# Graph attention in column tiles of 32: four narrow matmuls in place of one wide one, in a two-layer graph kernel

## The chip, the cores and the metric

The kernel runs on one core of a Trainium2 chip. The metric is the device time of one execution in microseconds, the median over a few runs. One execution is also taken with the hardware profiler; it gives the profile and the trace that this document reads.

## The reference

Two layers follow each other on a graph of N = 2708 nodes with 512 features. Only the first is touched here. It normalises x, takes the positive part h, and applies graph attention with 8 heads of 64 features over a dense adjacency matrix of zeros and ones. Cut to what matters:

```python
feats = jnp.einsum('nf,hfd->hnd', X, W)
e_self = jnp.einsum('hnd,hd->hn', feats, a_self)
e_neigh = jnp.einsum('hnd,hd->hn', feats, a_neigh)
dense = e_self[:, :, None] + e_neigh[:, None, :]
dense = jnp.where(dense >= 0, dense, LEAKY_ALPHA * dense)
dense = dense + (NEG_INF * (1.0 - A))[None, :, :]
attn = jax.nn.softmax(dense, axis=-1)
out = jnp.einsum('hnm,hmd->hnd', attn, feats) + b[:, None, :]
out = jnp.transpose(out, (1, 0, 2)).reshape(N, H * D)
return jax.nn.relu(out)
```

The layer's result is added to x. The second layer (graph diffusion in two steps, with a nucleus mask found by a search for thresholds) takes the larger part of the time and stays as it is.

## The kernel before

The nodes are cut into NT = 22 row tiles of 128 (the last has 20 rows). Everything that is multiplied here is f32.

**First stage.** Per row tile, x is normalised and projected. The tile `fw[:, t, head, :]` gets 65 columns for each head (DV = DH + 1): the 64 features times exp(e_neigh), and in the last column exp(e_neigh) itself, so that one matmul gives a head's weighted sum of features and the sum of its weights. `kk` holds exp(-0.8 e_neigh), and the tensor `en_d` in memory exp(0.8 e_self). A weight of the attention is then max(en, kk) times the adjacency, up to a factor that cancels.

**Attention.** The destination nodes are cut into chunks of whole row tiles, at most four (`tchunks`): six chunks, four of 512 columns, one of 384, one of 276. A chunk loads the share `r_b` of four heads at a time (line 345), broadcast to all partitions, and all 22 tiles of the transposed adjacency for its columns into `a_c` (line 434, f32, NT + 2 buffers). ScalarE copies each of them to `s_c` (line 439), which adds its row sums on the way and is stored to `s_d` for the second layer. For the nodes of the chunk, whole rows of the adjacency are loaded into `arow` and summed on ScalarE (`row_sums`, lines 338 and 339).

Then, for each of the two groups of four heads, for each row tile t, for each head of the group: VectorE writes the weights `e`, which are the larger of r_b and kk, times a_c (line 455, 10 buffers), and TensorE multiplies them into that head's bank of PSUM (line 457), accumulating over t:

```python
po = [ps_o.tile([P, 512], F32, name="po")[:DV] for _ in grp]
...
nc.tensor.matmul(po[i][:, :cw], lhsT=fw[:pr, t, hd, :], rhs=e[:pr, :cw],
                 start=(t == 0), stop=(t == NT - 1))
```

Six banks serve `po` and two the transposes. After the 22 tiles ScalarE copies the four banks to `o_t` (line 462), 65 partitions for each head.

**Finishing.** Each finished row tile of a chunk passes five stages (`finished`): `turned` transposes o_t per head (line 366), `shared` divides by the sums of weights, `normed` adds x and normalises, `cleared` takes the positive part, `asked` projects for the second layer (transposes on line 412, matmuls on line 175). These stages are put behind row tiles of the next chunk (`later`), one at a time, so that they run between its matmuls. The last chunk has no next one: its stages follow at the end (`final`), and the last of them is left to the beginning of the second layer.

**Order.** In this part the framework lays out each engine's order in advance; loads and stores are issued by SyncE in one queue, and each engine carries out its instructions in that order. Waits come from the tiles: an instruction that writes a buffer waits for the last reader of what stood there.

Of the kernel before, what the change touches and what calls it, by code (L numbers as in the profile page):

```python
# [9 lines left out]
F32 = mybir.dt.float32  # L10
BF16 = mybir.dt.bfloat16
# [13 lines left out]
P = 128  # L25
# [28 lines left out]
def kernel(  # L54
# [157 lines left out]
    NB = -(-NT // TG)  # L212
    tchunks = []
    for c in range(NB):
        t0 = tchunks[-1][-1] + 1 if c else 0
        tchunks.append(list(range(t0, t0 + NT // NB + (c < NT % NB))))
    with ExitStack() as l0:
# [110 lines left out]
        tp = l0.enter_context(tc.tile_pool(name="l0t", bufs=10))  # L328
# [14 lines left out]
        def shares(grp, n0, cw):  # L343
            r_b = rbp.tile([P, HG, 512], F32, name="r_b")
# [6 lines left out]
        def finished(t, o_t, c0, bank, final):  # L351
# [3 lines left out]
            f3 = fsum.rearrange("p (h d) -> p h d", h=H)  # L355
# [12 lines left out]
            def shared():  # L368
# [5 lines left out]
                for pn, grp in zip(pns, hgroups):  # L374
                    nc.vector.tensor_scalar(den[:pr, grp[0]:grp[-1] + 1], pn[:pr, :, DH],
                                            lone_n[:pr, t:t + 1], None, op0=OP.add)
                nc.vector.reciprocal(rden[:pr], den[:pr])
                for pn, grp in zip(pns, hgroups):
                    s = slice(grp[0], grp[-1] + 1)
                    nc.vector.scalar_tensor_tensor(o3[:pr, s, :], f3[:pr, s, :], lone[:pr, t:t + 1],  # L380
                                                   pn[:pr, :, :DH], op0=OP.mult, op1=OP.add)
# [44 lines left out]
        for ci, tiles in enumerate(tchunks):  # L426
# [1027 lines left out]
```

## Time and profile before

| what | us |
|---|---|
| median of 3 runs (lowest to highest) | 3573.36 (3570.47 to 3583.9) |
| the profiled execution | 3562.47 |
| its span in the trace | 3560.7 |
| TensorE busy, matmuls (10797 records) | 3332.0 (94%) |
| TensorE weight loads busy | 1729.1 (49%) |
| VectorE busy | 2650.8 (74%) |
| ScalarE busy | 1508.6 (42%) |
| GpSimd busy | 890.4 (25%) |
| transfers | 579.99 MB, mean 163 GB/s |

A line of the page's fifth part reads: source line, engine, operation, tile written, tiles read, shape, number; then busy us and mean ns of one; then the idle time of the engine just before such instructions, and what ended most of it. PE stands for matmuls, PEld for weight loads, DVE for VectorE, ACT for ScalarE, POOL for GpSimd, SP for SyncE. `128*65 128x512` at a matmul means 128 rows by 65 columns of weights, and 512 moving columns from 128 partitions. In the second part the span is cut into 40 slices of 89 us, and each digit is a busy share in tenths. Matmul records contain the time in which the array empties, so the records of successive matmuls overlap.

### The profile page before, as it was taken

The numbers are of one execution on the slowest core, as the hardware profiler recorded it, in microseconds if no ns is written. First come the engines' busy times: TensorE is split into PE (matmuls) and PEld (weight loads), VectorE is DVE, ScalarE is ACT, GpSimd is POOL, SyncE is SP. The second block draws the span as 40 slices with busy tenths as digits, with TensorE's granted clock in tenths as the row PEclk, the third lists the DMA queues.
The fourth block names the chain that finished last, engine by engine and source line by source line (L and its number), as shares of the span: only waits on it lengthen the run. The fifth ranks groups of instructions, "written<-read, shape, count | busy, mean of one in ns | idle before, by whom it ended". The sixth has DMA issues, their size and how long they took to land. (4 is left out here: it accounts for less than half of the span.)

```text
span 3560.7 us, 34129 instructions
## 1 busy us (share of the span) xinstructions
PE 3332.0 (94%) x10797; PEld 1729.1 (49%) x10797; DVE 2650.8 (74%) x4828; ACT 1508.6 (42%) x2269; POOL 890.4 (25%) x1074
## 2 busy tenths in 40 slices
PE   8999999998988999999999999899998999988998
PEld 4433333333455544646555554465555555555554
DVE  4587888889985756545464734598899998888883
ACT  2344211111103676566565642353655554545610
POOL 4114241415321121211222221311312332212211
PEclk9999999999999999999999999999999999999999
DMA  4476424242327624525344453695545535556453
GB/s 116 155 244 243 154 95 139 76 125 84 103 98 269 238 83 153 196 90 208 108 157 170 136 175 101 226 307 169 175 163 189 199 130 183 174 183 210 163 202 124
DMA packets 251348, 579.99 MB, mean 163 GB/s; under 512 B 33945, under 2 KB 76553, under 8 KB 248291
## 3 DMA queue, kind: packets, MB, share of 16 engines
q1 hardware_dynamic: 229063, 503.39, 42.7%
q0 software_dynamic: 22064, 74.09, 5.4%
q8 instruction: 86, 1.41, 0.2%
q14 instruction: 135, 1.11, 0.1%
HBM read 471.68 MB, written 105.68 MB: 162 GB/s over the span
## 5 line engine op out<-in xcount | busy, mean ns | idle before, releaser
L1140 PE MATMUL a<-va,at 128*128 128x512 f32 (+2 forms) x1936 | 887.1, 598 | 5.0 <-ACT at L1122 4.7
L457 PE MATMUL po<-e,fw 128*65 128x512 f32 (+4 forms) x2112 | 841.9, 554 | 28.8 <-DVE e L455 20.4
L455 DVE SCALAR_TENSOR_TENSOR e<-r_b,kk,a_c 128x512 f32<-128x512 f32 (+4 forms) x1056 | 750.4, 739 | 70.0 <-PE po L457 19.0
L576 ACT ACTIVATE junk_a<-p,nth 128x2708 uint8<-128x2708 f32 (+1 forms) x240 | 612.8, 2553 | 32.1 <-POOL nth L591 27.6
L1014 PE MATMUL q<-hl,s_r 128*128 128x512 f32 x1936 | 537.9, 424 | 63.3 <-DMA s_r<-s_d 45.3
L457 PEld LDWEIGHTS po<-e,fw 128*65 128x65 f32 (+1 forms) x2112 | 287.3, 140 | 543.5 <-issue 275.1
L1140 PEld LDWEIGHTS a<-va,at 128*128 128x128 f32 (+2 forms) x1936 | 338.3, 186 | 374.5 <-issue 341.9
L1014 PEld LDWEIGHTS q<-hl,s_r 128*128 128x128 f32 x1936 | 363.5, 192 | 225.9 <-issue 64.8
L1122 ACT COPY at<-t 128x512 f32<-128x512 f32 (+3 forms) x308 | 140.6, 478 | 655.8 <-PE t L1118 652.4
L655 DVE SCALAR_TENSOR_TENSOR junk<-p,th 128x2708 bf16<-128x2708 f32 (+1 forms) x132 | 407.2, 3085 | 3.0
L1034 PE MATMUL q<-u_k,v 128*128 128x512 f32 x704 | 316.9, 592 | 0.8 <-ACT v L1024 0.8
L1017 PE MATMUL q<-s_r,hl 128*128 128x512 f32 (+1 forms) x1056 | 282.3, 413 | 15.2 <-DMA s_r<-s_d 11.1
L1017 PEld LDWEIGHTS q<-s_r,hl 128*128 128x128 f32 x1056 | 196.0, 192 | 94.9 <-issue 51.6
L1034 PEld LDWEIGHTS q<-u_k,v 128*128 128x128 f32 x704 | 133.3, 190 | 158.6 <-issue 154.4
L544 ACT COPY p<-t 128x452 f32<-128x452 f32 (+2 forms) x264 | 131.3, 536 | 162.0 <-PE t L542 115.6
L542 PE MATMUL t<-keys,q_t 128*128 128x452 f32 x528 | 160.9, 432 | 41.2 <-ACT p L544 38.1
L851 DVE MAX8 vn<-keep 128x8 f32<-128x2708 f32 (+1 forms) x66 | 196.8, 2981 | 2.3
L569 DVE TENSOR_REDUCE nmx<-p 128x1 f32<-128x2708 f32 (+1 forms) x44 | 130.5, 2967 | 88.1 <-ACT p L544 88.1
L439 ACT ACTIVATE s_c<-a_c 128x512 fp32r<-128x512 f32 (+3 forms) x132 | 76.2, 577 | 249.0 <-DMA a_c<-in_adj_t_dram 122.3
L1187 PE MATMUL a<-u_k,v_t 128*128 128x512 f32 (+1 forms) x352 | 168.6, 619 | 5.2 <-ACT yo L1194 3.0
L1118 PEld LDWEIGHTS t<-ident,keep 128*128 128x128 f32 (+1 forms) x968 | 114.7, 139 | 76.1 <-issue 46.5
L1118 PE MATMUL t<-ident,keep 128*128 128x128 f32 (+1 forms) x968 | 145.3, 272 | 2.9 <-ACT p L544 2.8
(311 smaller groups left out, 3358.2 us busy)
## 6 DMA issues: line engine op xcount, KB each, us to landing
hl<-vhl_d SPq DMA_DIRECT2D x132, 512.0 KB
s_r<-s_d SPq DMA_DIRECT2D x264, 256.0 KB
hl<-fhl_d SPq DMA_DIRECT2D x132, 512.0 KB
hl<-bhl_d SPq DMA_DIRECT2D x132, 512.0 KB
u_k<-in_L_gnn_U_dram SPq DMA_DIRECT2D x184, 256.0 KB
arow<-in_adj_dram SPq DMA_DIRECT2D x21, 1354.0 KB
s_r<-s_d SPq DMA_DIRECT2D x132, 192.0 KB
s_d<-s_c SPq DMA_DIRECT2D x88, 256.0 KB
```

Of the source, the lines that this page charges most:

```text
L455: nc.vector.scalar_tensor_tensor(e[:pr, :cw], r_b[:pr, i, :cw], kk[:pr, t, hd:hd + 1], a_c[t][:pr, :cw], op0=OP.max, op1=OP.mult)
L457: nc.tensor.matmul(po[i][:, :cw], lhsT=fw[:pr, t, hd, :], rhs=e[:pr, :cw], start=(t == 0), stop=(t == NT - 1))
L542: nc.tensor.matmul(pl[:, :c1 - c0], lhsT=q[:, i], rhs=self.keys[:, c0:c1], start=(i == 0), stop=(i == 1))
L576: nc.scalar.activation(junk[:pr], self.p[i][:pr], func, **kw)
L655: nc.vector.scalar_tensor_tensor(self.junk_b[:pr], p, th, p, op0=OP.is_ge, op1=OP.mult, accum_out=dst)
L851: v.max(vs, keep[0][:pr])
L1014: nc.tensor.matmul(half[j], lhsT=s_r[:, j * P:(j + 1) * P], rhs=hl[:, h], start=(c == 0 and h == 0), stop=(c == NT - 1 and h == 1))
L1017: nc.tensor.matmul(half[j][:, :w], lhsT=hl[:, h, j * P:(j + 1) * P], rhs=s_r[:, :w], start=(c == 0 and h == 0), stop=(c == NT - 1 and h == 1))
L1034: nc.tensor.matmul(half[j], lhsT=across_t[-1][k][:, j * P:(j + 1) * P], rhs=u_k, start=(start and k == 0), stop=(start and k == KD - 1))
L1118: nc.tensor.transpose(pt[:rows[c], j, :pr], keep[i][:pr, cols[c]], ident[:pr, :pr])
L1140: nc.tensor.matmul(pa[:pr], lhsT=at[:rows[c], j, :pr], rhs=va[:rows[c], c, :], start=(c == 0), stop=(c == NT - 1))
L1187: nc.tensor.matmul(pz[i][:rows[t]], lhsT=v_t[i][:, k, :rows[t]], rhs=u_k, start=(k == 0), stop=(k == KD - 1))
```

## The change

The 65 weight columns of a head are taken apart. Its 64 features are two matmuls of 32 columns each, and its sum of weights a third of 32 columns, all equal (the one column of weights, broadcast). Each of them writes 32 partitions of a bank, at partition 0, 32, 64 or 96. For each row tile t two heads fill one bank with features (four matmuls), the other two heads a second, and the four sums a third. The chunks have six row tiles, 768 columns (`WC`), so that e is written 768 columns at a time; a matmul takes half of them, 384. There are four chunks, of 768, 768, 768 and 404 columns; in the last a matmul takes all 404. Chunk and group thus use all six banks of `po`.

To make room, e has 6 buffers of 768 in place of 10 of 512. The adjacency is loaded in f32 to `a_f` (3 buffers), and ScalarE copies it to `a_c` as bf16, which e is computed from. `arow` is loaded and summed in two halves, which GpSimd adds. Features of two heads now stand together in `o_t` (128 partitions), the sums in `o_d`, so that `turned` has four transposes of features and two of sums for a row tile, in place of eight. The stages of finished tiles are spread over both groups of the next chunk. The last chunk has four row tiles in place of three.

```diff
-    NB = -(-NT // TG)
-    tchunks = []
-    ...
+    TC = 6
+    WC = TC * P
+    tchunks = [list(range(t, min(t + TC, NT))) for t in range(0, NT, TC)]
+    NG = len(hgroups)
+    NPR = HG // 2
...
-        tp = l0.enter_context(tc.tile_pool(name="l0t", bufs=10))
+        tp = l0.enter_context(tc.tile_pool(name="l0t", bufs=6))
...
         def row_sums(t):
             pr = rows[t]
-            arow = adjp.tile([P, N], F32, name="arow", bufs=1)
-            nc.sync.dma_start(out=arow[:pr], in_=adj[cols[t], :])
-            nc.scalar.activation(arow[:pr], arow[:pr], AF.Copy, accum_out=rsum[:pr, t:t + 1])
+            half = small.tile([P, 2], F32, name="half")
+            w = -(-N // 2)
+            for i in range(2):
+                arow = adjp.tile([P, w], F32, name="arow", bufs=1)
+                c = slice(i * w, min((i + 1) * w, N))
+                arow = arow[:pr, :c.stop - c.start]
+                nc.sync.dma_start(out=arow, in_=adj[cols[t], c])
+                nc.scalar.activation(arow, arow, AF.Copy, accum_out=half[:pr, i:i + 1])
+            nc.gpsimd.tensor_tensor(rsum[:pr, t:t + 1], half[:pr, 0:1], half[:pr, 1:2], op=OP.add)
...
-            r_b = rbp.tile([P, HG, 512], F32, name="r_b")
+            r_b = rbp.tile([P, HG, WC], F32, name="r_b")
...
-                for g, grp in enumerate(hgroups):
-                    pn = bank(g)
-                    pns.append(pn[:, :HG * DV].rearrange("p (h d) -> p h d", h=HG))
-                    for i, hd in enumerate(grp):
-                        nc.tensor.transpose(pns[g][:pr, i, :], o_t[:, hd, c0:c0 + pr], ident[:DV, :DV])
+                for g, (src, n) in enumerate(((o_t, H // 2), (o_d, NG))):
+                    pns.append(bank(g).rearrange("p (k d) -> p k d", k=KD))
+                    for k in range(n):
+                        nc.tensor.transpose(pns[g][:pr, k, :], src[:, k, c0:c0 + pr], ident)
...
-                a_c.append(adjp.tile([P, 512], F32, name="a_c", bufs=NT + 2))
-                nc.sync.dma_start(out=a_c[t][:pr, :cw], in_=adj_t[cols[t], n0:n1])
-                s_c = small.tile([P, 512], F32R, name="s_c", bufs=4)
+                a_f = adjp.tile([P, WC], F32, name="a_f", bufs=3)
+                nc.sync.dma_start(out=a_f[:pr, :cw], in_=adj_t[cols[t], n0:n1])
+                a_c.append(adjp.tile([P, WC], BF16, name="a_c", bufs=NT + 2))
+                nc.scalar.copy(a_c[t][:pr, :cw], a_f[:pr, :cw])
+                s_c = small.tile([P, WC], F32R, name="s_c", bufs=3)
...
-            for grp, r_b in zip(hgroups, r_bs):
-                po = [ps_o.tile([P, 512], F32, name="po")[:DV] for _ in grp]
+            o_t = work.tile([P, H // 2, WC], F32, name="o_t", bufs=1)
+            o_d = work.tile([P, NG, WC], F32, name="o_d", bufs=1)
+            halfs = -(-cw // 512)
+            hw = -(-cw // halfs)
+            parts = [(a, min(a + hw, cw)) for a in range(0, cw, hw)]
+            for gi, (grp, r_b) in enumerate(zip(hgroups, r_bs)):
+                po = [[ps_o.tile([P, 512], F32, name="po") for _ in parts] for _ in range(NPR + 1)]
                 for t in range(NT):
                     pr = rows[t]
-                    for i, hd in enumerate(grp):
-                        e = tp.tile([P, 512], F32, name="e")
-                        nc.vector.scalar_tensor_tensor(e[:pr, :cw], r_b[:pr, i, :cw], kk[:pr, t, hd:hd + 1],
-                                                       a_c[t][:pr, :cw], op0=OP.max, op1=OP.mult)
-                        nc.tensor.matmul(po[i][:, :cw], lhsT=fw[:pr, t, hd, :], rhs=e[:pr, :cw],
-                                         start=(t == 0), stop=(t == NT - 1))
-                    for stage in later.pop(t, ()):
+                    es = []
+                    w = P // HG
+                    for k in range(NPR):
+                        for i in (2 * k, 2 * k + 1):
+                            hd = grp[i]
+                            e = tp.tile([P, WC], F32, name="e")
+                            es.append(e)
+                            nc.vector.scalar_tensor_tensor(e[:pr, :cw], r_b[:pr, i, :cw], kk[:pr, t, hd:hd + 1],
+                                                           a_c[t][:pr, :cw], op0=OP.max, op1=OP.mult)
+                        for n, (a, b) in enumerate(parts):
+                            for q in range(HG):
+                                i, d = 2 * k + q // 2, q % 2 * w
+                                nc.tensor.matmul(po[k][n][q * w:(q + 1) * w, :b - a],
+                                                 lhsT=fw[:pr, t, grp[i], d:d + w], rhs=es[i][:pr, a:b],
+                                                 start=(t == 0), stop=(t == NT - 1))
+                    for n, (a, b) in enumerate(parts):
+                        for i, hd in enumerate(grp):
+                            nc.tensor.matmul(po[NPR][n][i * w:(i + 1) * w, :b - a],
+                                             lhsT=fw[:pr, t, hd, DH:].to_broadcast([pr, w]), rhs=es[i][:pr, a:b],
+                                             start=(t == 0), stop=(t == NT - 1))
+                    for stage in later.pop(gi * NT + t, ()):
                         stage()
...
```

More of the change, by code (lines that the diff above doesn't have):

```diff
@@ L210 @@
     hgroups = [list(range(g, min(g + HG, H))) for g in range(0, H, HG)]
-    NB = -(-NT // TG)
-    tchunks = []
-    for c in range(NB):
-        t0 = tchunks[-1][-1] + 1 if c else 0
-        tchunks.append(list(range(t0, t0 + NT // NB + (c < NT % NB))))
+    TC = 6
[3 more added lines that the diff above has]
+    NPR = HG // 2
     with ExitStack() as l0:
@@ L349, in shares, with finished @@
             return r_b
-        def finished(t, o_t, c0, bank, final):
+        def finished(t, o_t, o_d, c0, bank, final):
             pr = rows[t]
-            f3 = fsum.rearrange("p (h d) -> p h d", h=H)
             pns, held = [], []
@@ L373, in shared @@
                 o3 = o.rearrange("p (h d) -> p h d", h=H)
-                for pn, grp in zip(pns, hgroups):
-                    nc.vector.tensor_scalar(den[:pr, grp[0]:grp[-1] + 1], pn[:pr, :, DH],
-                                            lone_n[:pr, t:t + 1], None, op0=OP.add)
+                pn, pd = pns
+                nc.vector.tensor_scalar(den[:pr], pd[:pr, :NG, ::P // HG].rearrange("p g i -> p (g i)"),
+                                        lone_n[:pr, t:t + 1], None, op0=OP.add)
                 nc.vector.reciprocal(rden[:pr], den[:pr])
[L378 to L381, printed above, removed]
+                nc.vector.scalar_tensor_tensor(o[:pr], fsum[:pr], lone[:pr, t:t + 1],
+                                               pn[:pr].rearrange("p k d -> p (k d)"), op0=OP.mult, op1=OP.add)
                 eng = nc.vector if final else nc.gpsimd
@@ L438 @@
                     nc.gpsimd.memset(s_c.bitcast(F32), 0.0)
-                nc.scalar.activation(s_c[:pr, :cw], a_c[t][:pr, :cw], AF.Copy,
+                nc.scalar.activation(s_c[:pr, :cw], a_f[:pr, :cw], AF.Copy,
                                      accum_out=cpart[:pr, t, ci:ci + 1])
@@ L447 @@
             r_bs += [shares(grp, n0, cw) for grp in hgroups[1:]]
-            o_t = work.tile([DV, H, 512], F32, name="o_t", bufs=1)
-            for grp, r_b in zip(hgroups, r_bs):
-                po = [ps_o.tile([P, 512], F32, name="po")[:DV] for _ in grp]
+            o_t = work.tile([P, H // 2, WC], F32, name="o_t", bufs=1)
[3 more added lines that the diff above has]
+            parts = [(a, min(a + hw, cw)) for a in range(0, cw, hw)]
@@ L460 @@
+                    for n, (a, b) in enumerate(parts):
[4 more added lines that the diff above has]
+                    for stage in later.pop(gi * NT + t, ()):
                         stage()
-                for i, hd in enumerate(grp):
-                    nc.scalar.copy(o_t[:, hd, :cw], po[i][:, :cw])
+                for k in range(NPR + 1):
+                    for n, (a, b) in enumerate(parts):
+                        to = o_t[:, gi * NPR + k, a:b] if k < NPR else o_d[:, gi, a:b]
+                        nc.scalar.copy(to, po[k][n][:, :b - a])
@@ L464 @@
             final = ci == len(tchunks) - 1
             for i, t in enumerate(tiles):
-                if final:
+                if final and i < 3:
                     bank = lambda g: ps_o.tile([P, 512], F32, name="po")
@@ L469 @@
                     bank = lambda g: ps_t.tile([P, 512], F32, name=f"pn{g}")
-                for n, stage in enumerate(finished(t, o_t, t * P - n0, bank, final)):
-                    later.setdefault(n if final else i * 5 + n, []).append(stage)
+                for n, stage in enumerate(finished(t, o_t, o_d, t * P - n0, bank, final)):
+                    later.setdefault(n if final else 3 * i + n + n // 4, []).append(stage)
         for n in sorted(later):
```

## The prediction

> **What bounds the kernel now.** I read the page first: its engine rows, the slices and the costliest groups. The change touches only graph attention, so I then cut out the stretch from the first matmul of line 457 (138.6 us) to the last (1044.3), and in it asked for sums by engine, groups by shape, and what line 457 waits for. The page:
>
> ```profile
> PE   8999999998988999999999999899998999988998
> DVE  4587888889985756545464734598899998888883
> PEclk9999999999999999999999999999999999999999
> L457 PE MATMUL po<-e,fw 128*65 128x512 f32 (+4 forms) x2112 | 841.9, 554 | 28.8 <-DVE e L455 20.4
> L455 DVE SCALAR_TENSOR_TENSOR e<-r_b,kk,a_c 128x512 f32<-128x512 f32 (+4 forms) x1056 | 750.4, 739 | 70.0 <-PE po L457 19.0
> ```
>
> TensorE and VectorE are both nearly full in slices 2 to 11. VectorE has 1056 instructions and TensorE 2112 records for as many matmuls: an f32 matmul runs as two passes, each with a weight load of its own. The stretch in sums (length, then busy PE, PEld, DVE, ACT, POOL, then the granted clock), and its main groups by shape (busy us, mean ns):
>
> ```profile
> 138.60:1044.30 905.70, 871.21 (x2492) 325.94 (x2492) 804.57 (x1257) 194.45 (x429) 270.27 (x340) 0.97 0.42 140
> L457 PE MATMUL po<-e,fw 128*65 128x512 f32 x1344 | 601.8, 605 | 15.3 <-DVE e L455 10.4 <-ACT o_t L462 4.8
> L455 DVE SCALAR_TENSOR_TENSOR e<-r_b,kk,a_c 128x512 f32<-128x512 f32 x671 | 517.6, 793 | 53.3 <-PE po L457 12.3
> L455 DVE SCALAR_TENSOR_TENSOR e<-r_b,kk,a_c 128x276 f32<-128x276 f32 x168 | 86.3, 567 | 1.5 <-PE po L457 0.3
> ```
>
> TensorE is busy 96%, VectorE 89%: PE is the limit with DVE close behind. The starts of successive 512-column passes lie 429 ns apart in the trace (323 at 384 columns, 233 at 276), so a pass [...]hands over with no gap; the record of 605 ns holds some 176 ns of drain besides. All columns: 2708 x 22 x 8 x 2 passes at 429/512 ns = 798 us of streaming. The other 107 us are small matmuls (22.0 + 13.4 + 12.1 us busy on lines 175, 366, 412), idle time and slices below full clock (0.97).
>
> **The matmuls.** For four heads and 512 columns there were four matmuls, eight passes on the whole array. Now twelve matmuls have 32 weight columns each; four that lie on different column tiles follow each other, three such rounds. If four share the array fully, streaming is 3/4 of 798 = 599 us. If none do it is 12/4 of it, 2394 us. No matmul of before shares the array with another, so the trace does not decide. Two rows bear on it. One is the gapless 429 ns: the second pass already stands at the array while the first streams. The other is the price of small passes, with 20 weight columns and 16 moving ones:
>
> ```profile
> 130.45 0.35 PE L294 MATMUL pe<-wa,h_t 128*20 128x16 f32 x8
> ```
>
> Eight passes with eight weight loads in 350 ns, 176 of them the last one's drain, so seven intervals in 174: 25 ns a pair. Twice 12 pairs for 384 columns cost 24 x 25 = 600 ns to issue, below the 3 x 2 x 323 = 1938 ns that the shared rounds stream, so issue does not bind.
>
> Here a rule speaks against the change. The Trainium skill, "TensorE: Matmul & The Clock Gate", Part 3, says that matmuls start and end in program order, "strict FIFO, no reordering". With two passes per matmul the order is tile 0 first pass, tile 0 second pass, tile 1 first pass. If the second pass holds up all behind it until its own tile is free, only one matmul's second pass runs beside the next one's first: each matmul costs one pass time, twelve cost 12 instead of 6, and streaming is 1.5 x 798 = 1197 us. "TensorEngine Tiling (Array Packing)", Key Properties, says instead that tiles operate independently and load and multiply in parallel, which gives 599. A hand-over without a gap needs a place where the next pass waits ready; one such place for each tile gives 599, one for the whole engine 1197. I take the first and keep the second as the main rival.
>
> **VectorE.** From 276 to 512 columns the mean rises by 226 ns: 0.958 ns a column and 303 fixed. So 768 columns cost 1.04 us, 404 cost 0.69. Instructions fall from 1056 to 704: 528 x 1.04 + 176 x 0.69 = 670 us, against 750. That in1 becomes bf16 I cost at nothing: bound from 0 to minus half the columns' time, taken at 0[...]. Chunks of six tiles give 384 + 384 columns per matmul; the last has 404 (four tiles).
>
> **The buffers of e decide the pace.** There are 6, four are used per row tile t, and all four are read until the last round of t. With full sharing: at the end T of round three of t-1 two e of t are ready, the other two can only be written now. PE does round one meanwhile (2 x 646 ns at 384 columns, 1.33 us at clock 0.97), then waits. The fourth e is ready after 2 x 1.04 plus 0.3 (0.18 of drain before the buffer counts as free, 0.1 from e to matmul): 2.38. Rounds two and three take 2.66. Period 5.04 us; VectorE works 4.16 of it, PE 3.99. For 404 columns: 1.38 + 0.3 + 2 x 0.70 = 3.08. Steps: 6 groups x 22 x 5.04 = 665, 2 x 22 x 3.08 = 136, **801 us**. The wait of PE for e, 210 us on the weight loads now and mostly covered, becomes real: about 1 us a step.
>
> What comes on top. The stages of finished tiles: VectorE has 804.6 - 749.5 = 55 us of them and waits 32 us for POOL in them, 4.6 us a tile over 19 tiles; behind each stands the next e. A step leaves 0.9 us free and a tile has five stages, so most is covered; I charge a quarter, 18 x 1.15 = 20. (Uncovered: 83.) The small matmuls, 47 us, run where PE waits for e: 10. Six banks are now all taken by a group, where two were spare; the first matmul of a group waits for copies of 0.5 us on ACT: 8 x 1.5 = 12. Start: r_b is 1.5 MB instead of 1, and a conversion of 0.85 us stands ahead of the first e: 3. Sum 846 us, against 905.7: **-60**. After the stretch, four finished tiles are uncovered instead of three, of which one had 20 rows; they follow at some 5 us (the projections of line 175 start at 1066.4 and 1073.2): +6. Net -54.
>
> **ScalarE and queues.** Its 2708-column rows (2553 ns) and 512-column rows (627) give 0.88 ns a column and 178 fixed: 0.85 us for a conversion, the same plus 187 for the sums of s_c. 66 steps x 1.9 + 22 x 1.3 = 154 us, where 100 stood; with row sums (now 44 halves, some 8 us more), copies (42 for 48) and the rest about 280 of 846: not a limit. But a_c is now made by ScalarE: its in-order queue has copies of o_t ahead of conversions, and behind a late row sum the next e would wait. In the compiled order the conversions of a chunk stand among those of the group before, so they run about 22 steps ahead; cost 0, uncovered 2 to 4 us per chunk, up to 16. SP carries fewer, larger transfers, the same bytes; arow comes in 44 halves, behind which a_f stands, and a_f has three buffers: 1.9 us of conversion per tile against 5.04 a step leaves room. POOL gets 22 one-column additions, under 1 us each, waited for only by the row sums. Transposes of o: 8 at 62 ns become 6 at 109, +0.15 us a tile, covered.
>
> **Sum.** The profiled execution took 3562.5 us (span 3560.7): 3562.5 - 54 = 3508. The median of the runs shown is 3573.4, 0.3% above it, so 3508 x 1.003 = 3519; I say **3518**. From no change about 0.5%, 18 us, can be told.
>
> **Rivals.**
> - *Passes in line* (slower). In-order second passes, place: the new feature and sum rounds; price: one pass time per matmul, 323/0.97 = 333 ns at 384 columns, 350 at 404: 132 x 24 x 0.333 + 44 x 12 x 0.350 = 1240, plus 47 small matmuls now uncovered, 12 and 3: 1302, +396 and +6 give 3965, and 3975 as a median; weight loads in line add 3696 x 25 ns = 92, up to 4065. It decides once fewer than about 2.9 matmuls share the array (2394/0.97/2.9 + 62 = 913). For it: two passes per matmul, and the rule. Against: the gapless hand-over, which shows a pass standing ready.
> - *No sharing*, the change does not do what it says: 2394/0.97 + 62 = 2530, +1625, about 5200. Against it: each tile has partitions and weights of its own.
> - *VectorE alone is the limit*, the e buffers cost nothing because round one overlaps: 670 + 55 + 32 = 757, -149 and +6, about 3430. Against it: six buffers for four in use.
> - *The cover fails*: conversions late, stages uncovered (63 more), so the 60 are given back: 3570 to 3600.
>
> **How the numbers follow.** Forecast, 3455 to 3565 with the stage cover at its ends: 0.47 (faster 0.43, same 0.03, slower 0.01). VectorE alone 0.07, faster. Passes in line 0.34, none shared 0.05, slower. Cover fails 0.07 (same 0.04, slower 0.03). Faster 0.50, same 0.07, slower 0.43. The range goes from 3440 to 4030: it holds the forecast, the failed cover and most of passes in line, about 0.8. The forecast's own range is 3455 to 3565.
>
> **What would show it.** Starts of successive passes in the new matmuls of po: four first passes within some 30 ns each and about 646 ns per round means full sharing; 323 ns from matmul to matmul means passes in line; 646 each means none. With sharing, these matmuls should wait for e about 1 us a step and the stretch last 846 us; VectorE's form with 768 columns should have a mean of 1.04 us. A stretch over 905 us, or PE without idle time in it, proves the forecast wrong.

## The result, and the profile after

| | us |
|---|---|
| before, median of 4 runs beside the changed kernel (lowest to highest) | 3578.05 (3570.47 to 3583.9) |
| after, median of 4 runs | 3513.21 (3508.41 to 3516.07) |
| ratio, 95% interval | 0.9819, 0.98 to 0.9838 |
| profiled execution after, its span | 3510.4, 3508.5 |

The change made the kernel 1.8% faster, 65 us of the medians. The page of the changed kernel, with the rows that answer to those of before (slices, then groups: busy us, mean ns, idle time before and what ended it):

```profile
PE   8998899899968999999999999889988999888998
...
DVE  4587889889937656474564653798989899878894
...
PEclk9999999999989999999999999999999999999999
...
L468 DVE SCALAR_TENSOR_TENSOR e<-r_b,kk,a_c 128x768 f32<-128x768 f32 (+3 forms) x704 | 667.7, 1004 | 86.4 <-PE po L478 80.2
L473 PE MATMUL po<-e,fw 128*32 128x384 f32 (+3 forms) x4928 | 609.6, 504 | 63.9 <-DVE e L468 43.9
...
L473 PEld LDWEIGHTS po<-e,fw 128*32 128x32 f32 (+1 forms) x4928 | 183.4, 110 | 384.1 <-DVE e L468 185.6
L478 PE MATMUL po<-e,fw 128*32 128x384 f32 (+3 forms) x2464 | 354.5, 493 | 0.0
```

L473 are the passes of the features and L478 those of the weights' sums. VectorE's e now waits 80 us for TensorE to free a buffer, and TensorE's weight loads 186 us for e: neither engine is full, each waits for the other. In slice 11, counted from 0, the tail of the finished tiles shows as a hole. The stretch from the first attention matmul to the last, as sums (length, then busy PE, PEld, DVE, ACT, POOL, then the granted clock):

```profile
139.70:965.20 825.50, 767.24 (x7716) 290.91 (x7716) 719.75 (x859) 240.41 (x462) 304.13 (x347) 0.98 0.44 150
```

It was 905.7 us. Where the time went, in the two profiled executions; the stretches meet one another, and "tail" is the time from the last attention matmul to the second layer's first search (the maximum of p):

| | before | after | difference | forecast |
|---|---|---|---|---|
| up to the first attention matmul | 138.6 | 139.7 | +1.1 | (in the 846) |
| attention stretch | 905.7 | 825.3 | -80.4 | -60 |
| tail | 50.6 | 65.8 | +15.2 | +6 |
| second layer | 2465.9 | 2477.6 | +11.7 | 0 |
| span | 3560.7 | 3508.5 | -52.2 | -54 |

The first three rows sum to -64, near the 65 us of the medians. The second layer, which the change leaves alone, is looked at in e5_before_e6.

**Do the four tiles share?** The timeline of the changed kernel (start us, busy us, engine, line, number of passes run together):

```profile
299.54 1.16 PE L473 MATMUL po<-e,fw 128*32 128x384 f32 x10
300.22 0.49 PE L478 MATMUL po<-e,fw 128*32 128x384 f32 x2
300.53 0.49 PE L473 MATMUL po<-e,fw 128*32 128x384 f32 x2
300.54 1.45 PE L478 MATMUL po<-e,fw 128*32 128x384 f32 x12
301.51 0.49 PE L473 MATMUL po<-e,fw 128*32 128x384 f32 x2
301.82 0.49 PE L478 MATMUL po<-e,fw 128*32 128x384 f32 x2
```

The single start times of L473 in the trace, in us, at a place where e is ready:

```
403.718  403.725  403.732  403.738
404.065  404.072  404.078  404.086
404.387  404.394  404.401  404.408
404.710  404.717  404.723  404.731
```

Four passes start within 20 ns, 7 ns apart, and the next four 322 ns later, the time of one pass over 384 columns. Sharing is complete, and the second passes hold nobody up. The lines at 300 us show more. In the program, also in the order laid out for the engine, all 32 feature passes of a row tile stand ahead of its 16 passes for the sums. On the chip passes of L478 start at 300.22, and passes of L473 that stand ahead of them at 300.53. Tiles 0 and 1 had come two passes ahead while tiles 2 and 3 had no e, and went on to their sums. Once its passes are issued, each column tile works off its own list.

An instruction that waits for its e does hold up those behind it, on other tiles too. In this step the third e ends at 298.553 us and the fourth at 299.480. The starts of L473 around that time (the first two of lines 1 and 2 are tiles 2 and 3, still with the second e, the last two tiles 0 and 1 with the third):

```
298.590  298.597  298.608  298.615
298.913  298.919  298.957  298.962
299.535  299.542  299.548  299.555
```

Tiles 0 and 1 start on the third e at 298.608 and 298.957. Their next passes, over the other half of the same e, stand in the program behind matmuls that need the fourth e, and start only with these, at 299.535 to 299.555. The weight loads show the wait:

```profile
299.53 0.16 PEld L473 LDWEIGHTS po<-e,fw 128*32 128x32 f32 x8 [0.78 <-DVE e L468]
```

**What a step costs.** VectorE's timeline in a group without stages of finished tiles:

```profile
297.54 3.80 DVE L468 SCALAR_TENSOR_TENSOR e<-r_b,kk,a_c 128x768 f32<-128x768 f32 x4 [0.39 <-PE po L478]
301.73 1.02 DVE L468 SCALAR_TENSOR_TENSOR e<-r_b,kk,a_c 128x768 f32<-128x768 f32 x1 [0.39 <-PE po L478]
```

Four e in 3.80 us and 0.39 us of waiting for a buffer: a step of 4.20 us, where 5.04 was forecast (2.28 instead of 3.08 at 404 columns). From the start of one group's first matmul to that of the next (the last one to the end of the stretch), the groups of 22 steps last, in us, in the order they run:

| columns | 768 | 768 | 768 | 768 | 768 | 768 | 404 | 404 |
|---|---|---|---|---|---|---|---|---|
| stages of finished tiles | no | no | six tiles | no | six | no | six | no |
| group | 100.2 | 103.1 | 142.1 | 94.5 | 139.9 | 94.6 | 100.6 | 50.3 |

The stages all stand in the first group of the next chunk, not in both as "The change" has it: the place `3 * i + n + n // 4` of a stage is at most 20, and a group has 22 steps. Each group with stages is compared with the one behind it: 47.6 + 45.3 + 50.3 = 143 us for 18 tiles, 8 us a tile. Before, the same comparison gives 73 us for 19 tiles, 3.8 us a tile, and 2.7 in its two middle groups (89.0 against 78.2 us for four).

VectorE's e in the second group with stages, and in the group behind it:

```profile
L468 DVE SCALAR_TENSOR_TENSOR e<-r_b,kk,a_c 128x768 f32<-128x768 f32 (+1 forms) x89 | 104.6, 1217 | 13.0 <-PE po L478 13.0
L468 DVE SCALAR_TENSOR_TENSOR e<-r_b,kk,a_c 128x768 f32<-128x768 f32 (+2 forms) x89 | 83.9, 1003 | 13.3 <-PE po L478 13.3
```

The waits for TensorE are as long with the stages as without (in the first such group longer, 18.9 against 10.7), so they covered nothing. On top come 21 us by which e take longer (104.6 against 83.9), 17 us of VectorE's other work and 6 us in which that work waits for GpSimd: 44 of the 45.3 us. In the kernel before, the stages did use up VectorE's idle time. In the groups of 89.0 and 78.2 us it idles before e for 0.7 us with stages and for 9.5 without:

```profile
L455 DVE SCALAR_TENSOR_TENSOR e<-r_b,kk,a_c 128x512 f32<-128x512 f32 (+1 forms) x84 | 69.2, 874 | 0.7 <-PE po L457 0.3
L455 DVE SCALAR_TENSOR_TENSOR e<-r_b,kk,a_c 128x512 f32<-128x512 f32 (+1 forms) x93 | 69.4, 752 | 9.5 <-PE po L457 0.8
```

### The profile page after: what moved, and what is told of

The parts are those of the page before. It is cut to its first block, busy times and chain, and to the rows that moved or that the text cites. A ratio compares the mean times of both kernels' runs of the same rounds, so it can differ in the third digit from the quotient of the medians.

```text
span 3508.5 us, 44409 instructions
## 1 busy us (share of the span) xinstructions
PE 3229.9 (92%) x16033; PEld 1694.5 (48%) x16033; DVE 2573.1 (73%) x4436; ACT 1556.4 (44%) x2307; POOL 931.8 (27%) x1091
## 5 line engine op out<-in xcount | busy, mean ns | idle before, releaser
L468 DVE SCALAR_TENSOR_TENSOR e<-r_b,kk,a_c 128x768 f32<-128x768 f32 (+3 forms) x704 | 667.7, 1004 | 86.4 <-PE po L478 80.2
L473 PE MATMUL po<-e,fw 128*32 128x384 f32 (+3 forms) x4928 | 609.6, 504 | 63.9 <-DVE e L468 43.9
L473 PEld LDWEIGHTS po<-e,fw 128*32 128x32 f32 (+1 forms) x4928 | 183.4, 110 | 384.1 <-DVE e L468 185.6
L478 PE MATMUL po<-e,fw 128*32 128x384 f32 (+3 forms) x2464 | 354.5, 493 | 0.0
L1041 PE MATMUL q<-s_r,hl 128*128 128x512 f32 (+1 forms) x1056 | 281.6, 412 | 28.5 <-DMA s_r<-s_d 22.0
L478 PEld LDWEIGHTS po<-e,fw 128*32 128x32 f32 (+1 forms) x2464 | 120.4, 111 | 118.1 <-issue 109.4
L154 POOL TENSOR_SCALAR ln_rs<-ln_mv 128x1 f32<-128x1 f32 x66 | 49.4, 749 | 411.1 <-DVE ln_mv L153 410.6
```

Of the source, the lines that this page charges most:

```text
L468: nc.vector.scalar_tensor_tensor(e[:pr, :cw], r_b[:pr, i, :cw], kk[:pr, t, hd:hd + 1], a_c[t][:pr, :cw], op0=OP.max, op1=OP.mult)
L473: nc.tensor.matmul(po[k][n][q * w:(q + 1) * w, :b - a], lhsT=fw[:pr, t, grp[i], d:d + w], rhs=es[i][:pr, a:b], start=(t == 0), stop=(t == ...
L478: nc.tensor.matmul(po[NPR][n][i * w:(i + 1) * w, :b - a], lhsT=fw[:pr, t, hd, DH:].to_broadcast([pr, w]), rhs=es[i][:pr, a:b], start=(t == ...
L1041: nc.tensor.matmul(half[j][:, :w], lhsT=hl[:, h, j * P:(j + 1) * P], rhs=s_r[:, :w], start=(c == 0 and h == 0), stop=(c == NT - 1 and h == 1))
```

## The experiments

One table first; the columns are explained below it.

| kernel | median us | ratio | stretch | step | stages | tail |
|---|---|---|---|---|---|---|
| after | 3513.2 | 0.9819 (0.98 to 0.9838) | 825.3 | 4.20 | 143 | 65.8 |
| e1_tilemajor | 3507.4, one run | | 823.1 | 3.88 | 152 | 65.6 |
| e2_e8 | 3481.5 | 0.9727 (0.9699 to 0.9756) | 795.6 | 3.87 | 136 | 64.9 |
| e3_t512 | 3626.1 | 1.0131 (1.0099 to 1.0163) | 946.1 | 2.58 | | 51.6 |
| e4_tail | 3509.6 | 0.9803 (0.9778 to 0.9829) | 826.0 | | | 64.1 |
| e5_before_e6 | 3581.2, one run | | 914.0 | 3.43 | | 52.1 |
| e6_t512_e6 | 3532.3 | 0.9864 (0.9824 to 0.9903) | 849.9 | 2.75 | | 53.2 |
| e7_t512_noadd | 3576.8, one run | | 898.1 | 2.58 | | 50.7 |
| e8_rows | 3473.2 | 0.9714 (0.968 to 0.9747) | 798.7 | 3.87 | 135 | 64.3 |
| e9_relief | 3476.1 | 0.9725 (0.9699 to 0.975) | 786.8 | 3.87 | 133 | 63.4 |
| e10_quarters | 3486.7 | 0.9731 (0.9708 to 0.9753) | 799.5 | 3.87 | 132 | 62.9 |
| e11_best | 3480.4 | 0.9727 (0.9707 to 0.9748) | 793.5 | 3.87 | 126 | 65.3 |
| e12_split | 3445.9 | 0.9645 (0.9622 to 0.9667) | 760.3 | 3.87 | 96 | 64.8 |

The ratio is to runs of the kernel before on the same chip (medians 3574 to 3580). Stretch, step (the commonest, at 768 columns; at 512 in e3, e5, e6 and e7), stages (surplus of the three groups with stages over the group behind each) and tail are from the profiled execution, in us; the stages of the kernels without a number were not compared. e7_t512_noadd leaves out an addition that the second layer needs, so only its stretch can be compared.

**e1_tilemajor: all of a tile's matmuls one after another.**

```diff
-                        for n, (a, b) in enumerate(parts):
-                            for q in range(HG):
+                        for q in range(HG):
+                            for n, (a, b) in enumerate(parts):
```

(and the same for the sums)

> The changed kernel, with another order of the same matmuls: the two halves of a chunk follow each other on one column tile before the next tile gets any, so in program order a tile has four passes before the next has its first. Nothing else moves. Theory 'a queue for each tile, several deep': passes wait at their tile and hold up nobody else; a row tile's step without stages stays at 4.2 us, the attention stretch at 825 us (within 10), the total near 3510. Rival 'one pass waits at each tile': a third pass holds up everything behind it until the second has started, so each tile starts 0.65 us after the one before; a step takes about 7.7 us, the stretch about 1290, the total about 3970.

If a tile held one waiting pass and the rest stood in one common line, this order would cost most. It costs nothing: a step fell from 4.20 to 3.88 us, which is six rounds, three for each half of the columns, of 0.645 us for two passes. So several instructions wait ready at each tile, not one. The step is shorter than the theory asked for, because both halves of an e now stand ahead of the matmuls that need the next one, and the stop before the fourth e is gone. The kernel gained little: the groups with stages stayed at 142 and 141 us, and TensorE's gaps at the ends of the first two groups grew from 5.5 and 5.7 to 12.4 and 13.8 us.

**e2_e8: two more buffers for e.** a_f and s_c give up one each to make room.

```diff
-        tp = l0.enter_context(tc.tile_pool(name="l0t", bufs=6))
+        tp = l0.enter_context(tc.tile_pool(name="l0t", bufs=8))
...
-                a_f = adjp.tile([P, WC], F32, name="a_f", bufs=3)
+                a_f = adjp.tile([P, WC], F32, name="a_f", bufs=2)
...
-                s_c = small.tile([P, WC], F32R, name="s_c", bufs=3)
+                s_c = small.tile([P, WC], F32R, name="s_c", bufs=2)
```

> The changed kernel with 8 buffers of e in place of 6; to make room a_f has 2 and s_c 2. Theory 'six buffers set the pace and leave the stages of finished tiles uncovered': a step without stages falls from 4.20 us to 3.9 (what the passes stream), and the stages' price falls from 7.9 us a tile towards the 2.7 of before; the stretch falls from 825 to 725-765, the total to 3420-3450. Rival 'the stages cost what their own waits cost': steps fall to 3.9, the groups with stages keep their surplus of 47 us; stretch about 785, total about 3470. Rival 'adjacency late': with fewer buffers of a_f the conversions come late and nothing is gained, total 3505 or more.

The step fell to 3.87 us and the stretch by 30 us. So six buffers cost 0.33 us a step in the changed kernel, and not about 1. They do it only together with its order of matmuls: e1_tilemajor reaches the same step with six. The stages kept nearly their whole price (136 us): that is not a matter of buffers.

**e3_t512: the column tiles alone**, in chunks of at most 512 columns as before, a_c in f32 and loaded straight, ten buffers for e, and a stage of a finished tile behind every row tile, as before.

```diff
-    TC = 6
+    TC = 4
...
-        tp = l0.enter_context(tc.tile_pool(name="l0t", bufs=6))
+        tp = l0.enter_context(tc.tile_pool(name="l0t", bufs=10))
...
-                nc.scalar.copy(a_c[t][:pr, :cw], a_f[:pr, :cw])
```

> Column tiles alone: matmuls as in the changed kernel, but the chunks of before (four of 512 columns, 384, 276), adjacency in f32 straight from memory without a conversion, 10 buffers of e of 512 columns, three finished tiles at the end. Theory 'sharing the array and cover for the stages are what counts': VectorE's four e take 2.65 us a step, the passes 2.57; a step about 2.75 us for 512 columns, stages 2.7 us a tile as before; stretch about 740, the end as before, total about 3395. Rival 'the wide chunk carries the gain': the fixed cost of narrow e and the wait for their buffers bring a step to 3.4, what it was before; stretch about 890, total about 3545.

The theory fell. Its steps are even shorter than it asked for, 2.58 us against 3.43 before, and yet the kernel is slower than before. The groups with stages hold one very long step each, of 68.9, 54.9, 28.5 and 18.0 us in the first four. The first one, in the timelines of this kernel by engine (GpSimd, VectorE, ScalarE), and TensorE's groups with their waits (window of that group):

```profile
216.15 46.80 POOL L449 TENSOR_TENSOR s_c<-s_c,ident 128x128 fp32r<-128x128 f32 x1 [6.43 <-ACT s_c L445]
262.91 0.19 POOL L349 TENSOR_TENSOR rsum<-half 128x1 f32<-128x1 f32 x1
```

```profile
212.87 49.76 DVE L470 SCALAR_TENSOR_TENSOR e<-r_b,kk,a_c 128x512 f32<-128x512 f32 x75
```

```profile
266.22 0.63 ACT L445 ACTIVATE s_c<-a_c 128x512 fp32r<-128x512 f32 x1 [46.13 <-DMA a_c<-in_adj_t_dram]
```

```profile
L374 PE MATMUL pn<-ident,o_t 128*128 128x128 f32 x16 | 3.4, 312 | 64.4 <-ACT o_t L488 64.4
```

Read from the top: GpSimd's small addition of the diagonal into s_c, whose median in this kernel is 0.45 us, lasts 46.8 us. VectorE writes 75 e in a row without one pause, and GpSimd ends 0.3 us after VectorE stops (212.87 + 49.76 = 262.63, and 262.95). The store of s_c, at the head of SyncE's queue, waits for it; the loads of a_c stand behind that store; ScalarE's next copy waits 46 us for its load, with the copies out of the accumulators behind it; and TensorE's transposes wait 64 us for those copies. The new theory: a VectorE that never pauses keeps GpSimd out of SBUF, the memory on the chip that both work on. Two runs were made to break it.

**e6_t512_e6: one number, fewer buffers.**

```diff
-        tp = l0.enter_context(tc.tile_pool(name="l0t", bufs=10))
+        tp = l0.enter_context(tc.tile_pool(name="l0t", bufs=6))
```

> Column tiles in chunks of 512, as in e3_t512, with one number changed: 6 buffers for e instead of 10, which alone can only make VectorE wait more. Theory: the 155 us of single stalls in e3_t512 come from a VectorE that runs e after e without a gap and keeps GpSimd out of SBUF until its next pause; with 6 buffers VectorE has to wait for TensorE in every step, GpSimd gets in, the 46.8 us of GpSimd's s_c addition goes back to about 1 us and the stalls of 69, 55 and 29 us go. Steps lengthen from 2.58 to 2.6 to 2.9 us (176 of them: up to 55 us), so the stretch goes from 946 to between 800 and 860 us and the kernel from 3626 to 3480 to 3540 us. Rival: the stalls come from the loads of the next chunk behind one another in SyncE's queue, whatever VectorE does; then they stay, the steps lengthen too, and the kernel takes 3626 to 3680 us.

Taking four buffers away made the kernel 94 us faster. The steps lengthened to 2.75 us, because VectorE now waits in each, and GpSimd got through. The same line of code in this kernel (ns, least, median and longest):

```profile
L449 POOL TENSOR_TENSOR s_c<-s_c,ident x22: 375/708/998, 138.2 to 884.0; 128x128 fp32r<-128x128 f32 x21, 20x20 fp32r<-20x20 f32 x1
```

No addition took over 1 us, and the longest steps are 15.6 and 19.6 us.

**e7_t512_noadd: ten buffers, without the addition.**

```diff
-                if t in tiles:
-                    d = slice(t * P - n0, t * P - n0 + pr)
-                    nc.gpsimd.tensor_tensor(s_c[:pr, d], s_c[:pr, d].bitcast(F32), ident[:pr, :pr], op=OP.add)
```

> e3_t512 with its 10 buffers, and without GpSimd's addition of the diagonal into the chunk's copy for layer 2 (it leaves the self loops out of that matrix, so only the attention stretch is read). Theory as for e6_t512_e6, from the other side: VectorE still runs without a gap, but nothing that the loads of the next chunk wait for runs on GpSimd, so the stall of 69 us goes; GpSimd's other work (row sums, stages of finished tiles) is still kept out, so part of the loss may show up elsewhere. Stretch 946 to between 790 and 880 us. Rival (loads in SyncE's queue, GpSimd's 46.8 us only the consequence of a late load): unchanged at about 946 us.

The stretch fell by 48 us, to above the range, and the first long step is still there, 72.6 us. GpSimd, VectorE and ScalarE in this kernel:

```profile
183.97 76.86 POOL L349 TENSOR_TENSOR rsum<-half 128x1 f32<-128x1 f32 x1 [10.31 <-ACT arow L348]
260.91 0.23 POOL L350 TENSOR_SCALAR lone<-rsum 128x1 f32<-128x1 f32 x1
```

```profile
169.26 91.50 DVE L467 SCALAR_TENSOR_TENSOR e<-r_b,kk,a_c 128x512 f32<-128x512 f32 x138
```

```profile
206.16 0.60 ACT L485 COPY o_d<-po 128x512 f32<-128x512 f32 x1
260.86 1.33 ACT L348 ACTIVATE arow<-arow 128x1354 f32<-128x1354 f32 x1 [54.10 <-POOL rsum L349]
```

That the stall would go with the addition was wrong; that GpSimd waits for VectorE fits again. An addition of one number per partition, 0.19 us by itself, was held for 76.9 us, until 0.07 us after VectorE's run of 138 e ended (169.26 + 91.50 = 260.76, and 260.83). Here it is another small piece of GpSimd's work that is caught, the row sum: ScalarE's next row sum needs a buffer that this addition reads, waits 54.1 us for it, and keeps everything of the next chunk behind it.

**e4_tail: the loads of x for the last tiles from ScalarE's queue.**

```diff
-                nc.sync.dma_start(out=xt[:pr], in_=x[cols[t], :])
+                (nc.scalar if final else nc.sync).dma_start(out=xt[:pr], in_=x[cols[t], :])
```

> The changed kernel; only the loads of x for the finished tiles of the last chunk are issued by ScalarE in place of SyncE. Theory 'head of SyncE's queue': the fourth such load waits 10.5 us for one of three buffers, and the second layer's loads of s_r and hl stand behind it; away from there they come at once, the time from the last attention matmul to the second layer's first reduction falls from 66 us to about 55, the total by 8 to 12 us. Rival 'the stages of four tiles on VectorE and GpSimd set the end': no change beyond 3 us.

In the tail of the changed kernel TensorE waits 9.43 us for a load of s_r, which the head of SyncE's queue kept back:

```profile
987.14 3.75 PE L1041 MATMUL q<-s_r,hl 128*128 128x512 f32 x8 [9.43 <-DMA s_r<-s_d]
```

With that cleared, the tail fell by 1.7 us only: the rival, the chain of four tiles' stages, fits. All kernels with three last tiles (e3, e5, e6, e7) have tails of 51 to 53 us, all with four 63 to 66, so the 15 us go with the fourth tile.

**e5_before_e6: the kernel before with six buffers for e.**

```diff
-        tp = l0.enter_context(tc.tile_pool(name="l0t", bufs=10))
+        tp = l0.enter_context(tc.tile_pool(name="l0t", bufs=6))
```

> The kernel before with 6 buffers for e instead of 10, one look, for two questions. First, layer 2: it took 2465.9 us in the one trace of before and 2476 to 2478 us in every trace of a changed kernel of 768 columns. If the change makes layer 2 longer, this trace shows 2466 again; if the traced execution of before happened to be a short one, it shows about 2477. Second, buffers: if the loop before is set by TensorE (steps of 3.43 us against 2.95 us of VectorE), two buffers of lookahead beyond the four in use are enough between stages and the attention stretch stays within 10 us of 905.7; stages of finished tiles may cost up to 5 us a tile more than the 2.7 us they cost there. Rival: buffers set the pace before too, and every step grows by 0.2 us or more, the stretch by 30 us or more.

The second layer took 2475.1 us with the old attention too. So the 11.7 us of the result's table are, as far as one execution tells, no effect of the change: the profiled execution of before was a short one (3562.5 us, where the median of its runs is 3578). The loop kept its 3.43 us and the stretch grew by 8 us: six buffers are enough there.

**e8_rows: a chunk's row sums spread over its loop.** In e2_e8 TensorE stands still for 12.0 and 14.5 us at the ends of the first two groups.

```diff
-            for t in tiles:
-                row_sums(t)
...
+                    if (gi * NT + t) % 6 == 5 and (gi * NT + t) // 6 < len(tiles):
+                        row_sums(tiles[(gi * NT + t) // 6])
```

> e2_e8 (3481 us) with the row sums of a chunk's tiles issued one at every sixth step of the loop instead of all ahead of it. In e2_e8 TensorE has two gaps in the first chunk, 12.0 us at 228.2 and 14.5 us at 327.2: ScalarE's copies out of the finished group's accumulators (L486) stand in its queue behind row sums (L344) that wait for their loads. Theory: issued later, each row sum finds its load done, both gaps go, and small gains come in the later chunks: stretch 795.6 to 765 to 772 us, kernel 3452 to 3462 us. Rival: the gaps are the accumulators' alone (a group starts only when six are copied) and come back as waits for L486 of the same length: no change, 3478 to 3485 us.

The theory fell: the gaps stayed, 13.5 and 16.1 us, and the time is that of e2_e8 within both intervals. ScalarE at the end of the first group of this kernel:

```profile
238.81 1.33 ACT L344 ACTIVATE arow<-arow 128x1354 f32<-128x1354 f32 x1 [4.09 <-DMA arow<-in_adj_dram]
240.05 0.19 ACT L344 ACTIVATION_READ_ACCUMULATOR arow<-arow 128x1 f32 x1
240.14 1.60 ACT L486 COPY o_t<-po 128x384 f32<-128x384 f32 x4
```

Row sums still stand there ahead of the copies (L486): the framework lays out ScalarE's order by its own estimates, and another place in the code did not change it here.

**e10_quarters: the rows in quarters, in two buffers.**

```diff
-            half = small.tile([P, 2], F32, name="half")
-            w = -(-N // 2)
-            for i in range(2):
-                arow = adjp.tile([P, w], F32, name="arow", bufs=1)
+            half = small.tile([P, 4], F32, name="half")
+            w = -(-N // 4)
+            for i in range(4):
+                arow = adjp.tile([P, w], F32, name="arow", bufs=2)
...
-            nc.gpsimd.tensor_tensor(rsum[:pr, t:t + 1], half[:pr, 0:1], half[:pr, 1:2], op=OP.add)
+            nc.scalar.activation(half[:pr], half[:pr], AF.Copy, accum_out=rsum[:pr, t:t + 1])
```

> e2_e8 with the rows for the row sums loaded in quarters into two buffers of the same total size instead of in halves into one, and the parts added by ScalarE's own accumulation instead of by GpSimd. e8_rows showed that moving the row sums in the code leaves the gaps at the first two group ends (13.5 and 16.1 us) where they are, because two row sums still wait for their loads ahead of ScalarE's copies. Theory: with a load ahead the row sum does not wait, and the gaps shrink to 3 to 6 us each: stretch 795.6 to 773 to 783 us, kernel 3460 to 3470 us. Rival: the loads are limited by SyncE's queue, not by the one buffer, and twice as many loads make the gaps as long or longer: 3478 to 3495 us.

The rival was right: the gaps grew to 18.6 and 17.8 us. How to order these loads so that the copies are not behind them was not tried further.

**e9_relief: two pieces of the stages moved to ScalarE** (on e2_e8).

```diff
+                if final:
+                    eng.tensor_mul(o3[:pr], o3[:pr], rden[:pr].unsqueeze(2).to_broadcast([pr, H, DH]))
+                else:
+                    for hd in range(H):
+                        nc.scalar.activation(o3[:pr, hd], o3[:pr, hd], AF.Copy, scale=rden[:pr, hd:hd + 1])
...
-                nc.vector.tensor_scalar(o[:pr], o[:pr], mean, rs, op0=OP.subtract, op1=OP.mult)
-                nc.scalar.activation(v[:pr], o[:pr], AF.Relu)
+                nm = small.tile([P, 1], F32, name="nm")
+                nc.scalar.mul(nm[:pr], mean, -1.0)
+                nc.scalar.activation(o[:pr], o[:pr], AF.Identity, bias=nm[:pr])
+                nc.scalar.activation(v[:pr], o[:pr], AF.Relu, scale=rs)
```

> e2_e8 (3481 us, stretch 795.6) with two pieces of a finished tile's stages moved to ScalarE, which is busy a third of the time: the division by the weights' sums (GpSimd, 1.49 us a tile) as eight scaled copies, and the normalisation (VectorE, 0.55 us a tile and a wait of 0.5 us for GpSimd before it) as two activations. Theory of the stages' cost: a tile costs 7.9 us because VectorE, which sets the pace together with TensorE, does 4.6 us of its own work for it and, while GpSimd works on SBUF beside it, runs slower (its e took 1.28 us on average among stages, 1.01 elsewhere, which is 24 us per six tiles). Then 1.05 us go on VectorE and about 1.2 us of slowed e, 2.2 us a tile, 31 us over the 14 tiles that are not last: stretch 760 to 770 us, kernel 3445 to 3458 us. Rival: the cost is TensorE's waits for the transposes and for ScalarE's copies, which get more behind them on ScalarE now: stretch 790 to 810, kernel 3476 to 3495 us.

Both were half right. In a group with stages, e took 1.28 us on average in e2_e8 and 1.09 here, as the theory had it. But the stretch fell by 9 us only. TensorE's groups in the third group of steps, and ScalarE's timeline in it, both of this kernel:

```profile
L175 PE MATMUL pn<-v_t,kw 128*128 128x128 f32 x40 | 7.6, 349 | 18.2 <-ACT v_t L422 18.2
```

```profile
377.71 0.72 ACT L412 ACTIVATE o<-o,nm 128x512 f32<-128x512 f32 x1
382.47 0.72 ACT L413 ACTIVATE v<-o,ln_rs 128x512 f32<-128x512 f32 x1 [4.03 <-POOL ln_rs L155]
383.09 0.57 ACT L422 COPY v_t<-pn 128x512 f32<-128x512 f32 x1
```

ScalarE waits 4 us for GpSimd's small steps of the normalisation, the copy of v_t of another tile stands behind that, and TensorE, in order, waits 18.2 us in this group for such copies. What VectorE gave up came back as a wait in a queue.

**e11_best: e9_relief, e10_quarters and e1_tilemajor together.**

> The parts together: e2_e8, the passes tile by tile of e1_tilemajor (worth 2 to 3 us there), the ScalarE pieces of e9_relief (31 us by theory) and the quarters of e10_quarters (15 us by theory). If the parts add, 3481 - 3 - 31 - 15 = 3432 us, 3425 to 3445; if both rivals hold, 3475 to 3500 us.

The parts do not add, and 3480 us lies where the rivals put it: the quarters' longer gaps (20.5 and 15.8 us) are in it, and the wait for v_t too (12.6 us in its third group).

**e12_split: e9_relief, with a tile's projection three steps later.**

```diff
                 nc.scalar.copy(v_t[:, :, :pr], pt[:, :, :pr])
+                held.append(v_t)
                 split_rows(halves, nc.gpsimd, v[:pr], t, vhl_d)
-                project(halves, bank(1), v_t, t, 0, bufs=2)
+
+            def projected():
+                project(halves, bank(1), held[5], t, 0, bufs=2)
...
-                    later.setdefault(n if final else 3 * i + n + n // 4, []).append(stage)
+                    later.setdefault(n if final else 3 * i + n + n // 4 + 2 * (n // 5), []).append(stage)
```

> e9_relief with the projection of a finished tile (L175 and what follows it) issued three steps after the tile's second transposes instead of right after them. In e9_relief VectorE's e among stages fell from 1.28 to 1.09 us as its theory said, but TensorE, in order, then waited for ScalarE's copy of v_t (18.2 us in one group of stages, single waits up to 7.5 us), because that copy stands behind activations that wait for GpSimd and VectorE. Theory: with three steps (11.6 us) between, the copy is done when the projection comes up, the waits go in the groups with 768-wide stages and the relief shows: 15 us in each of two groups and 5 us in the third, stretch 786.8 to 748 to 760 us, kernel 3476 to 3438 to 3450 us. Rival: the wait only moves on, to the next transposes, which need the same bank and the same ScalarE copy: stretch 780 to 795, kernel 3468 to 3485 us.

The theory held, at the edge of its range: stretch 760.3 us. TensorE's groups in the third group of steps, now:

```profile
L175 PE MATMUL pn<-v_t,kw 128*128 128x128 f32 x40 | 5.8, 288 | 0.0
L370 PE MATMUL pn<-ident,o_t 128*128 128x128 f32 x24 | 3.9, 286 | 6.7 <-ACT v_t L422 6.7
```

The projections wait for nothing; 6.7 of the 18.2 us moved on to the next transposes, as the rival said. The stages now cost 96 us, where e9_relief has 133 and the changed kernel 143. This kernel, 3446 us, is the fastest of all: 3.6% under the kernel before, and some 67 us under the changed one.

## Why the prediction was right, and where it was right by luck

3518 us were forecast and 3513 measured. The mechanism that decides it held. Two terms of the sum were far off, one by 146 us too much and the other by 113 too little; that they cancelled was luck, and either alone would have put the forecast off by over 100 us.

- *Sharing.* "One such place for each tile" was right: starts 7 ns apart, and tile-by-tile order loses nothing. The rule against it (the Trainium skill, "TensorE: Matmul & The Clock Gate", Part 3, strict order of matmuls) does not hold across column tiles in this trace, where passes of L478 start at 300.22 us and passes of L473 that stand before them at 300.53. That was the choice that decided the sign; its rival would have given 3975.
- *Streaming and VectorE.* e at 768 columns was forecast at 1.04 us, and its records last 1.09 on average. But the forecast took the length of a record for the distance of two: records overlap, and outside the stages e start 0.93 us apart, so that all e together cover 668 us (forecast 670). There they were cheaper than forecast, among stages dearer. That bf16 for in1 changes nothing was not tested by itself, but the 0.93 us show no gain from it: e of 512 columns, all f32, follow each other in 0.66 us in e7_t512_noadd (91.50 us for 138), so 256 more columns cost about 1 ns each with bf16, as the f32 columns did in the forecast (0.958).
- *The pace of the buffers: mis-sized.* "PE does round one meanwhile, then waits" let a round start only when all of its e are there. But tiles 0 and 1 run ahead of tiles 2 and 3. They begin round two with the third e, 0.93 us before the fourth (298.608 and 299.535 us above), and they end a row tile's sums 0.63 us before the others, which frees two buffers of e early. With e 0.93 us apart besides, VectorE waits 0.39 us a step. Steps of 4.20 and 2.28 us make 655 us of the stretch, not 801.
- *The stages: mis-sized the other way.* 20 us, "a quarter" of 83, and 10 for small matmuls. They cost 143, near the 83 + 47 called uncovered. The cover was taken to be the 0.9 us that VectorE waits in a step of 5.04; in a step of 4.20 it waits 0.39, and even that covered nothing (13.0 us of waits with stages, 13.3 without). Why VectorE goes on waiting for TensorE there was not shown. What the sum left out is e made longer: in the changed kernel's trace, the e of 768 columns that lie beside no GpSimd arithmetic took 1011 ns on average (338 of them), and those beside 0.6 us of it or more 1264 ns (138). e9_relief, which takes work from GpSimd and VectorE, agrees.
- *Group boundaries and start.* 12 and 3 us forecast; 825.3 - 655 - 143 leaves 27, of which 18 lie in the first two groups, where ScalarE's copies stand behind row sums. "ScalarE and queues: 0" overlooked that.
- *Tail.* +6, measured +15: not the loads (e4_tail), but, by the comparison of tails, a fourth tile's chain.
- *Rivals.* "VectorE alone is the limit" gave 3430. e12_split is near that, but with stages moved and with more buffers, which the rival did not ask for. "The cover fails" was true of the stages; its 3570 to 3600 us did not come, because the steps were shorter than the sum had them.

## What to carry to other kernels

An engine's waits in a step are no cover for other work by themselves: before, the stages used them up, after, the waits stayed and the stages came on top. Where matmuls wait for data that arrive one after another, put those whose data are there ahead of those that wait. Look out for a VectorE that runs e after e without a pause where anything on the way of a load or a copy runs on GpSimd; here a kernel with fewer buffers was the faster one. When work is moved to an idle engine, look at what stands behind it in that engine's queue, and give the consumer a few steps of distance before judging the move.

## What the runs showed of the hardware

- Column tiles of 32 run independently and start out of program order against one another: four passes 7 ns apart, each tile several instructions deep (300.22 and 300.53 us in the changed kernel, and the step of 3.88 us in e1_tilemajor). A matmul that waits for its data holds up those behind it on all tiles (no start between 298.962 and 299.535 us).
- A short GpSimd instruction can last as long as VectorE goes on without a pause. A page of the Trainium skill ("SBUF — State Buffer", section "SBUF: two separate sides") says that a VectorE operation with two SBUF inputs and a GpSimd operation that reads SBUF exclude each other for the length of an instruction. The exclusion agrees with the runs, though none shows the memory's ports themselves; the length does not: 46.8 us over some 70 e in e3_t512, 76.9 us over more than 100 in e7_t512_noadd. In e6_t512_e6, with its pauses, the addition that took 46.8 us takes at most 1 us. The same happened in the last group of e2_e8, where it hit nothing that others waited for (GpSimd, then VectorE):

```profile
887.55 47.43 POOL L187 TENSOR_TENSOR kq_hl<-kq_hl 128x128 f32<-128x128 f32 x1
```

```profile
882.53 52.13 DVE L468 SCALAR_TENSOR_TENSOR e<-r_b,kk,a_c 20x404 f32<-20x404 f32 x92
```

In other places GpSimd got in between two e, one short operation of 0.8 to 1.2 us at a time. What decides between the two was not found out.
